# A four-layer graph attention kernel: five small edits in its last layer

## The chip, the cores and the metric

The kernel runs on one core of a Trainium2 chip. The metric is the time of one execution in microseconds of the device. Before the change the median of four runs is 2012.05 us (2011.6 to 2016.34).

A core has engines with a queue of instructions each, worked off in order: PE (matrix products), DVE (VectorE, element-wise), ACT (ScalarE, activations), POOL (GpSimd) and SP (only starts transfers here). They meet through semaphores. A transfer is started by an instruction in the queue of SP, ACT or POOL, and is then carried by 16 DMA engines.

## The reference

x is 4096 nodes by 256 features, adj a 4096 by 4096 matrix of zeros and ones with about 17 ones in a row. Four layers follow each other, each of the form

```python
x = layernorm(x + gat(x, adj, weights))
```

Layers 0 to 2 are graph attention with 4, 4 and 2 heads. Layer 3, the only one that the change touches, is

```python
h = x @ W
e = leaky_relu(h @ a[:256] + (h @ a[256:]).T, 0.2)
attention = softmax(where(adj > 0, e, -1e12))
negative = -softmax(where(adj > 0, -e, -1e12))
new = concatenate([attention @ x, negative @ x], axis=1) @ fc_W
x = layernorm(x + elu(new))
```

## The kernel before

**Two kinds of rows.** The 4096 rows are 32 tiles of 128. A first stage has turned adj into lists of the nodes that a tile's rows are joined to. In layer 3 the tiles 0 to 24 (`self.order`) go by such lists, "listed tiles" here: the values of the listed nodes, 516 numbers a node (two heads of 257, and two more), are gathered from DRAM by GpSimd, one indirect DMA for 128 nodes (`RowTile.load`, L802), and the masked weights are multiplied with them. The tiles 28 to 31 and then 25 to 27 (`WHOLE[3]`) go over all 4096 nodes instead, "all-node rows": `Layer.whole_rows`.

**A listed tile** has two halves. Half 0 takes its own rows (loaded by SP, L797) and 6 gathers, half 1 takes 7. A half is done by `RowTile.half`: ACT makes relu and two exponentials (L879, L880, L882), DVE masks the two weight tiles (L881 for head 1, then L883 for head 0), PE multiplies (L933). Its lists are of two sorts: a list in `FULL` serves all 128 rows of the tile, of the two lists of an entry in `PAIRS` one serves the first 64 rows and the other the last 64, and their matmuls run side by side on the left and the right half of the array. Half 0 has 1 full list and 3 pairs, half 1 has 3 full lists and 2 pairs. Each f32 matmul is two passes in the trace, so a half is 28 passes in both cases. The order of half 0 of layer 3 is: head 1 full, head 1 pairs, head 0 full, head 0 pairs. The buffers for the gathered rows (`g0`, `g1`, four each) hold two tiles in layer 3, so the gathers of half h of tile m wait until half h of tile m-2 has been multiplied. The last tile's half 1 is done list by list in `last_half` (L943 to L950).

**All-node rows** are worked off in units: one unit is one block of 128 nodes and one head for the 4 or 3 tiles of a group; SP loads the block's values (`vw`, L1193), ACT and DVE make the weights (`pw`, L1208 to L1213), PE has 4 or 3 matmuls (L1216). Layer 3 has 128 units, 64 for each group; 10 (`AHEAD`) are done while layer 2 ends, the others are spread by `Layer.whole` over the half steps (`step` counts halves of listed tiles, 50 in all, `count` is 25):

```python
while self.between is None and self.used < self.total \
        and self.used < self.ahead + (self.total - self.ahead) * (step + 1) / (2 * self.count - 6):
    self.unit()
```

After its last unit a group's tiles are finished one by one (`finish`, L1381 to L1389: division, elu, residual), each with its features loaded by `load_x` just then.

**The norm** (`norm`, L1318 to L1349) gathers tiles into a group (`GROUPS`) and takes the inverse root for the whole group: by three Newton steps on DVE (14 small operations), or, if the tile is the last listed one, by one `pow` on GpSimd (L1331). Tiles are normed in the order in which they are finished, listed and all-node ones mixed: a group of 25 and 23 comes, then one of 26, 27 and 24.

**Stores.** `scale` puts finished rows into `self.outs`; `store_rows` (L1094) starts their stores from ACT's queue. `half_with_whole` calls it in each half step after that half's first exponential, if something waits there, and `close` calls it before and after the last tile's `finish`.

**The order of the instructions** on an engine is not that of the Python text: a scheduler in the framework places each instruction by its own estimate, so an edit may move instructions that it does not name. The engines keep that order strictly.

Of the kernel before, what the change touches and what calls it, by code (L numbers as in the profile page):

```python
# [50 lines left out]
P = 128  # L51
N = 4096
F = 256
NT = N // P
# [4 lines left out]
JG = 8  # L59
# [20 lines left out]
FULL = ((0,), tuple(range(NPAIR - FIRST, NPACK - FIRST)))  # L80
PAIRS = (tuple(range(1, 1 + FIRST)), tuple(range(NPAIR - FIRST)))
# [680 lines left out]
class RowTile:  # L762
# [77 lines left out]
    def half(self, half):  # L840
        L, n, nc = self.layer, self.layer.n, self.layer.nc
        prog, sh, S = L.prog, L.shared, self.S
        H, Wd, V, T, A = HEADS[n], WIDTH[n], VALS[n], TERMS[n], LOGS[n]
# [3 lines left out]
        accs, U = self.accs, UNITS[half]  # L847
# [72 lines left out]
            turns = ((3, 0), (1, 2)) if n < 2 else ((0,), (1,))  # L920


        for t, heads in enumerate(turns):
            for us in (FULL[half], PAIRS[half])[::-1 if t == 1 and (half == 1 or n < 3) else 1]:
                for h in heads:
                    for u in us:
                        for rows, g in parts[u]:
                            a = accs[h][rows, :Wd] if n == 3 else accs[0][rows, h * Wd:(h + 1) * Wd]
                            b = g[:, h * Wd:(h + 1) * Wd]
                            if n < 2:  # L930
                                a = accs[0][rows, h * Wd:(H + 1) * Wd].rearrange("p (s c) -> p s c", c=Wd)[:, ::H - h]
                                b = b.rearrange("p (s c) -> p s c", s=1).to_broadcast([P, 2, Wd])
                            nc.tensor.matmul(a, w[h][:, u, rows], b,  # L933
                                             start=half == 0 and u == 0 and (n == 3 or h == turns[0][0]),
                                             stop=half == 1, skip_group_check=True)

    def last_half(self, accs, parts, w, mh):

# [21 lines left out]
class Layer:  # L960
# [39 lines left out]
    def whole(self, step):  # L1000

        while self.between is None and self.used < self.total \
                and self.used < self.ahead + (self.total - self.ahead) * (step + 1) / (2 * self.count - 6):
            self.unit()
        if self.used == self.total:
            next(self.units, None)
# [83 lines left out]
        self.stored = projs  # L1090

    def store_rows(self):
        for y, m in self.outs:
            self.nc.scalar.dma_start(out=self.prog.out[m * P:(m + 1) * P, :], in_=y)  # L1094
        self.outs = []

    def steps(self):
# [13 lines left out]
    def close(self, following):  # L1111

        last = self.count - 1
        self.step += 2
        for proj in self.stored:
            proj.store()
        if self.middle is not None:
            self.middle.values()
            self.middle.edge()
            self.middle.store()  # L1120
        for entry in [e for e in self.ready if e[2] < MIX]:
            self.ready.remove(entry)
            self.set_banks()
            Projection(self.prog, self.n + 1, self.nxt, *entry[1:]).all()
        if following is not None:
            for m in range(4 if following.n == 3 else 2 if WHOLE[self.n] else 1):
                following.load(m, 0)
        if WHOLE[self.n]:
            for _ in self.units:
                pass  # L1130
            if following is None:
                self.store_rows()
                self.tile(last).finish()
                self.store_rows()
                return


            self.closing = True
            following.ahead = AHEAD
            self.project_ready()  # L1140
            for _ in range(3):
                following.unit()
            self.tile(last).finish()
            scaled = self.scaled
            proj = self.project_ready()
            with ExitStack() as order:
                for ins in (scaled, proj.last):
                    order.enter_context(self.prog.tc.issue_after(ins.ins))
                following.tile(0).half(0)
                for _ in range(AHEAD - 3):  # L1150
                    following.unit()
                following.tile(1).half(0)
        else:
            self.set_banks()
            first = Projection(self.prog, self.n + 1, self.nxt, *self.ready.pop(0)[1:])
            first.transpose()
            following.tile(0).half(0)
            first.copy()
            first.multiply()
            first.values()  # L1160
            self.tile(last).finish()
            first.edge()
            first.store()
        self.project_ready()
        if following is not None:
            for m in (1, 2):
                following.load(m, 0)
            if not WHOLE[self.n]:
                following.tile(1).half(0)
            following.load(3, 0)  # L1170


    def whole_rows(self):
        n, nc, prog, sh = self.n, self.nc, self.prog, self.shared
        H, Wd, T = HEADS[n], WIDTH[n], TERMS[n]
        groups = [range(H)] if n < 3 else [(0,), (1,)]
        for tiles in WHOLE[n]:
            g = len(tiles)
            S = prog.bk.tile([P, T, BT, P], F32, name="Sw")
            for it, m in enumerate(tiles):  # L1180
                nc.sync.dma_start(out=S[:, :, it, :], in_=sh["e"][n][m].partition_broadcast(P))
            bits = self.block_bits(tiles)
            zs = [None] * g
            for heads in groups:
                accs = [prog.bank(prog.pfour) for _ in range(g)]
                c0, c1 = heads[0] * Wd, (heads[-1] + 1) * Wd
                vs = {}

                def fetch(j):
                    if j >= NT:  # L1190
                        return
                    vs[j] = prog.vp.tile([P, c1 - c0], F32, name="vw")
                    nc.sync.dma_start(out=vs[j], in_=sh["v"][n][0][j * P:(j + 1) * P, c0:c1])  # L1193

                for j in range(4):
                    fetch(j)
                for j in range(NT):
                    fetch(j + 4)
                    mj = self.bytes(bits, j)
                    v = vs.pop(j)  # L1200
                    for h in heads:
                        p = prog.dp.tile([P, BT, P], F32, name="pw")[:, :g]
                        d = sh["d"][n][:, j, h if n < 3 else 0:h + 1 if n < 3 else 1]
                        if n < 3:
                            nc.scalar.activation(p, S[:, h, :g], AF.Exp, bias=d)  # L1205
                            nc.vector.scalar_tensor_tensor(p, p, LEAST, mj, op0=ALU.max, op1=ALU.mult)  # L1206
                        else:
                            nc.scalar.activation(p, S[:, 0, :g], AF.Relu, bias=d)  # L1208
                            if h == 0:
                                nc.scalar.activation(p, p, AF.Exp, bias=sh["shift2"])  # L1210
                            else:
                                nc.scalar.activation(p, p, AF.Exp, scale=-1.0)  # L1212
                            nc.vector.tensor_tensor(p, p, mj, op=ALU.mult)  # L1213
                        c = h * Wd - c0
                        for it in range(g):
                            nc.tensor.matmul(accs[it][:, c:c + Wd], p[:, it, :], v[:, c:c + Wd],  # L1216
                                             start=(j == 0 and h == heads[0]), stop=(j == NT - 1),
                                             skip_group_check=True)
                    if n == 3 and heads[0] == 0 and j == NT - 1:
                        def between(accs=accs):  # L1220
                            for it in range(g):
                                zs[it], last = self.positive(accs[it], whole=True)
                            return last
                        self.between = between
                    yield
            for it, m in enumerate(tiles):
                self.finish(m, accs[it], self.load_x(m), zs[it])
                if n == 3:
                    yield

# [80 lines left out]
    def norm(self, y, m):  # L1311
# [13 lines left out]

        v = ep.tile([P, BT], F32, name="v")[:, :g]
        nc.vector.tensor_scalar(v, mv[:, :, 1], EPS, None, op0=ALU.add)
        if self.n == 3 and m == self.order[-1]:

            r = ep.tile([P, BT], F32, name="r")[:, :g]  # L1330
            nc.gpsimd.tensor_tensor(r, v, self.shared["mhalf"][:, :g], op=ALU.pow)  # L1331
            self.scale(mv, r)
            return
# [518 lines left out]
```

## Time and profile before

| what | us |
|---|---|
| median of four runs | 2012.05 |
| the profiled execution, its time | 2022.25 |
| the span of its trace (first to last instruction) | 2020.5 |
| first gather of layer 3 in the trace | 1544.72 |
| last gather of layer 3 | 1987.38 |
| last GpSimd operation (the `pow`) | 2007.78 |
| last DVE operation ends | 2009.77 |

Times below are microseconds from the start of the span of the profiled execution, which took 10.2 us more than the median of the runs. In a line of the trace, "L933" is a line of the kernel, PEld is PE's loading of weights, a letter q behind an engine's name (POOLq) means its queue alone was at work, and the brackets at the end give the time that the engine stood idle before and what released it. The view of groups gives busy time, mean nanoseconds of one instruction, and idle time before them. The chain of waits goes back from the last instruction to what released each step.

### The profile page before, as it was taken

Reading aid. Unit: us, or ns where it says so; the run is one execution under the profiler, and the core shown is the slowest. Engines: PE = TensorE matmul, PEld = TensorE weight load, DVE = VectorE, ACT = ScalarE, POOL = GpSimd, SP = SyncE. Lnnn points to the kernel's source line nnn. Section 1 sums busy time; section 2 is a strip of 40 time slices with the busy share of each in tenths; the row PEclk is TensorE's granted clock in tenths of the full one; section 3 lists DMA queues with packets and bytes.
Section 4 is the critical chain, followed back from the end, with each engine's and each line's share of the span. In section 5 each row is a group of like instructions: output and inputs, shape, how many; then the busy total and the mean of one; then the engine's idle time right before and its main releaser. Section 6 shows DMA issues by size and latency. Waiting matters only on the chain. (4 is left out here: it accounts for less than half of the span.)

```text
span 2020.5 us, 46645 instructions
## 1 busy us (share of the span) xinstructions
PE 1776.3 (88%) x15137; PEld 1456.2 (72%) x15137; DVE 1543.9 (76%) x5130; ACT 1494.5 (74%) x4705; POOL 1418.4 (70%) x1413
## 2 busy tenths in 40 slices
PE   5758889988999699999998889798988999999994
PEld 3537677777777589888776688788876777766672
DVE  3458888888888699988887878787866577686765
ACT  4659888899878577876677778777774688777763
POOL 0067777777777777777777777777763777777772
PEclk7759899999999899999999999899998999999997
DMA  8799999999756766666666657667765888898883
GB/s 300 224 337 315 313 288 283 294 296 297 227 170 196 198 175 187 179 185 167 183 171 181 187 160 196 183 188 210 201 184 155 245 274 257 269 294 276 279 264 103
DMA packets 294057, 459.20 MB, mean 227 GB/s; under 512 B 90982, under 2 KB 206795, under 8 KB 293804
## 3 DMA queue, kind: packets, MB, share of 16 engines
q0 software_dynamic: 76544, 233.01, 39.6%
q1 hardware_dynamic: 212642, 218.92, 35.1%
q10 hardware_dynamic: 4618, 4.20, 0.6%
q8 instruction: 122, 2.00, 0.4%
q14 instruction: 131, 1.07, 0.2%
HBM read 407.14 MB, written 48.81 MB: 226 GB/s over the span
## 5 line engine op out<-in xcount | busy, mean ns | idle before, releaser
L802 POOL DMA_INDIRECT G<-vals,idx x1378 | 1413.0, 1025 | 569.8 <-issue 350.7
L933 PE MATMUL bank<-G,w 128*64 128x130 f32 (+5 forms) x9268 | 939.9, 306 | 72.3 <-DVE w L869 66.7
L912 ACT ACTIVATE w<-S,G 128x64 f32<-128x64 f32 (+1 forms) x3108 | 833.9, 351 | 149.5 <-DMA G<-vals,idx 143.2
L933 PEld LDWEIGHTS bank<-G,w 128*64 128x64 f32 (+1 forms) x9268 | 756.1, 157 | 235.1 <-DVE w L869 82.5
L1216 PE MATMUL bank<-vw,pw 128*128 128x129 f32 (+1 forms) x2304 | 375.6, 319 | 19.4 <-ACT zw L1364 4.9
L1216 PEld LDWEIGHTS bank<-vw,pw 128*128 128x128 f32 x2304 | 332.9, 192 | 57.3 <-issue 15.9
L869 DVE SCALAR_TENSOR_TENSOR w<-w,bank 128x1024 f32<-128x1024 f32 (+1 forms) x240 | 322.7, 1345 | 12.9 <-ACT w L912 11.1
L696 PE MATMUL bank<-wext,xT 128*128 128x268 f32 (+3 forms) x640 | 190.3, 433 | 26.7 <-ACT xT L687 25.4
L879 ACT ACTIVATE w<-S,G 128x64 f32<-128x64 f32 (+1 forms) x343 | 108.9, 352 | 77.6 <-DMA G<-vals,idx 59.7
L696 PEld LDWEIGHTS bank<-wext,xT 128*128 128x128 f32 x640 | 125.1, 213 | 53.3 <-ACT xT L687 28.2
L404 ACT ACTIVATE mk<-raw 128x1024 uint8<-128x1024 int32 x128 | 129.6, 1048 | 26.3 <-DMA raw<-in_adjB_dram 25.1
L1206 DVE SCALAR_TENSOR_TENSOR pw<-pw,mw 128x512 f32<-128x512 f32 (+1 forms) x192 | 120.9, 642 | 30.3 <-ACT pw L1205 28.3
L1205 ACT ACTIVATE pw<-Sw,d 128x512 f32<-128x512 f32 (+1 forms) x192 | 126.4, 675 | 15.1 <-PE bank L1216 8.0
L908 DVE TENSOR_TENSOR w<-S,G 128x384 f32<-128x384 f32 x180 | 91.0, 508 | 41.7 <-DMA G<-vals,idx 36.9
L1213 DVE TENSOR_TENSOR pw<-pw,mw 128x512 f32<-128x512 f32 (+1 forms) x128 | 79.1, 621 | 53.4 <-ACT pw L1210 32.1
L1277 PE MATMUL bank<-vw,pw 128*128 128x65 f32 x512 | 89.3, 257 | 15.1 <-DVE pw L1274 15.1
L1279 PE MATMUL bank<-pw,vw 128*65 128x128 f32 x512 | 99.0, 276 | 0.0
L1277 PEld LDWEIGHTS bank<-vw,pw 128*128 128x128 f32 x512 | 78.1, 193 | 23.9 <-issue 21.0
L1208 ACT ACTIVATE pw<-Sw,d 128x512 f32<-128x512 f32 (+1 forms) x128 | 82.9, 655 | 14.9 <-DVE y L1349 6.4
L1274 DVE SCALAR_TENSOR_TENSOR pw<-Sw,cw,mw 128x512 f32<-128x512 f32 x128 | 92.8, 740 | 0.0
L687 ACT COPY xT<-bank 128x256 f32<-128x256 f32 x128 | 45.6, 358 | 57.2 <-PE bank L682 37.5
L914 DVE SCALAR_TENSOR_TENSOR w<-w,mk 128x512 f32<-128x512 f32 (+1 forms) x84 | 62.7, 751 | 23.6 <-ACT w L912 23.5
(197 smaller groups left out, 1912.0 us busy)
## 6 DMA issues: line engine op xcount, KB each, us to landing
raw<-in_adjB_dram SPq DMA_DIRECT2D x128, 512.0 KB
G<-vals,idx POOLq DMA_INDIRECT x1378
vw<-vals SPq DMA_DIRECT2D x128, 128.5 KB
S<-edge SPq DMA_DIRECT2D x60, 256.0 KB
vw<-vals SPq DMA_DIRECT2D x96, 129.0 KB
xp<-y SPq DMA_DIRECT2D x96, 128.0 KB
y<-xp SPq DMA_DIRECT2D x96, 128.0 KB
vals<-row SPq DMA_DIRECT2D x64, 152.0 KB
```

The lines of the kernel that those rows point to most:

```text
L404: nc.scalar.activation(self.mk[:, 2 * q:2 * q + 2], src, AF.Copy)
L696: nc.tensor.matmul(pp[:, :c1 - c0], self.xT[:, k, :], wext[:, k, c0:c1], start=(k == 0), stop=(k == KT - 1 and brow is None))
L802: nc.gpsimd.indirect_dma_start(out=self.row(half, k), out_offset=None, in_=self.values[:N + 1 if half else MIX * P, :].rearrange("r (k c) ...
L869: return nc.vector.scalar_tensor_tensor(pair, pair, LEAST, mh2, op0=ALU.max, op1=ALU.mult)
L879: nc.scalar.activation(w[0][:, u, rows], S[:, 0, rows], AF.Relu, bias=d(g, 0))
L912: nc.scalar.activation(w[h][:, u, rows], S[:, h, rows], AF.Exp, bias=d(g, h))
L933: nc.tensor.matmul(a, w[h][:, u, rows], b, start=half == 0 and u == 0 and (n == 3 or h == turns[0][0]), stop=half == 1, skip_group_check=True)
L1205: nc.scalar.activation(p, S[:, h, :g], AF.Exp, bias=d)
L1206: nc.vector.scalar_tensor_tensor(p, p, LEAST, mj, op0=ALU.max, op1=ALU.mult)
L1216: nc.tensor.matmul(accs[it][:, c:c + Wd], p[:, it, :], v[:, c:c + Wd], start=(j == 0 and h == heads[0]), stop=(j == NT - 1), skip_group_ch ...
L1277: nc.tensor.matmul(bu[:, it * Wd:(it + 1) * Wd], p[up][:, it, :], v[:, up * Wd:(up + 1) * Wd], start=j == 0 and it == 0, **how)
L1279: nc.tensor.matmul(bf[:Wd, it * P:(it + 1) * P], v[:, flat * Wd:(flat + 1) * Wd], p[flat][:, it, :], start=j == 0 and it == 0, **how)
```

## The change

Five things change:

- In `half`, half 0 of layer 3 multiplies head 1 full, head 0 full, head 1 pairs, head 0 pairs. All other halves keep their order.
- In `whole`, the divisor for layer 3 is `2 * count - 8` in place of `2 * count - 6`: its units are used up two half steps sooner.
- In `whole_rows`, the features of a group's tiles are loaded 8 units before the group's end, not at the finish.
- In `norm`, the `pow` on GpSimd is taken for the last two listed tiles, 23 and 24, with what stands in the group with them.
- In `store_rows`, every second store goes by SP's queue when `closing` is set; `close` now sets it for the last layer too.

```diff
-        for t, heads in enumerate(turns):
-            for us in (FULL[half], PAIRS[half])[::-1 if t == 1 and (half == 1 or n < 3) else 1]:
-                for h in heads:
+        runs = [(us, heads) for t, heads in enumerate(turns) for us in (FULL[half], PAIRS[half])[::-1 if t else 1]]
+        if n == 3 and half == 0:
+            runs = [(us, heads) for us in (FULL[0], PAIRS[0]) for heads in turns]
+        for us, heads in runs:
+            for h in heads:
...
-                and self.used < self.ahead + (self.total - self.ahead) * (step + 1) / (2 * self.count - 6):
+                and self.used < self.ahead + (self.total - self.ahead) * (step + 1) / (2 * self.count - (8 if self.n == 3 else 6)):
...
     def store_rows(self):
-        for y, m in self.outs:
-            self.nc.scalar.dma_start(out=self.prog.out[m * P:(m + 1) * P, :], in_=y)
+        for k, (y, m) in enumerate(self.outs):
+            queue = self.nc.sync if self.closing and k % 2 else self.nc.scalar
+            queue.dma_start(out=self.prog.out[m * P:(m + 1) * P, :], in_=y)
...
             for _ in self.units:
                 pass
+            self.closing = True
             if following is None:
                 self.store_rows()
                 self.tile(last).finish()
                 self.store_rows()
                 return
-
-
-            self.closing = True
...
-            zs = [None] * g
+            zs, ys = [None] * g, []
...
+                    if heads == groups[-1] and j == NT - JG:
+                        ys = [self.load_x(m) for m in tiles]
...
-                self.finish(m, accs[it], self.load_x(m), zs[it])
+                self.finish(m, accs[it], ys[it], zs[it])
...
-        if self.n == 3 and m == self.order[-1]:
+        if self.n == 3 and m in self.order[-2:]:
```

More of the change, by code (lines that the diff above doesn't have):

```diff
@@ L920, in half @@
             turns = ((3, 0), (1, 2)) if n < 2 else ((0,), (1,))
-        for t, heads in enumerate(turns):
-            for us in (FULL[half], PAIRS[half])[::-1 if t == 1 and (half == 1 or n < 3) else 1]:
-                for h in heads:
[L926 to L935, printed above, removed]
+        runs = [(us, heads) for t, heads in enumerate(turns) for us in (FULL[half], PAIRS[half])[::-1 if t else 1]]
[3 more added lines that the diff above has]
+            for h in heads:
+                for u in us:
+                    for rows, g in parts[u]:
+                        a = accs[h][rows, :Wd] if n == 3 else accs[0][rows, h * Wd:(h + 1) * Wd]
+                        b = g[:, h * Wd:(h + 1) * Wd]
+                        if n < 2:
+                            a = accs[0][rows, h * Wd:(H + 1) * Wd].rearrange("p (s c) -> p s c", c=Wd)[:, ::H - h]
+                            b = b.rearrange("p (s c) -> p s c", s=1).to_broadcast([P, 2, Wd])
+                        nc.tensor.matmul(a, w[h][:, u, rows], b,
+                                         start=half == 0 and u == 0 and (n == 3 or h == turns[0][0]),
+                                         stop=half == 1, skip_group_check=True)
     def last_half(self, accs, parts, w, mh):
```

## The prediction

> **What bounds the kernel now.** Only layer 3 is in question: up to it the compiled order of both programs is the same on every engine. I read first the busy time by stages. Columns: us, then busy (x instructions) of PE, PEld, DVE, ACT, POOL, PE's clock, DMA share, GB/s.
>
> ```profile
> 1720.00:1760.00 40.00, 40.00 (x217) 30.35 (x216) 26.93 (x92) 27.54 (x64) 29.01 (x30) 1.00 0.87 267
> 1800.00:1840.00 40.00, 39.88 (x222) 29.04 (x220) 28.19 (x111) 30.64 (x73) 30.59 (x31) 1.00 0.89 283
> 1990.00:2010.50 20.50, 4.31 (x17) 1.78 (x12) 16.01 (x73) 4.91 (x14) 0.89 (x1) 0.74 0.10 33
> ```
>
> PE looks like the bound until 1960, and after 1990 DVE works almost alone for 20 us. But POOL's groups, asked for before and after 1770, tell more:
>
> ```profile
> L802 POOL DMA_INDIRECT G<-vals,idx x123 | 127.3, 1035 | 43.7 <-issue 28.6 <-PE bank L933 4.9 <-ACT w L879 3.8
> L802 POOL DMA_INDIRECT G<-vals,idx x166 | 168.8, 1017 | 50.6 <-issue 38.7 <-DMA G<-vals,idx 4.0 <-PE bank L933 3.4
> ```
>
> Idle time for each gather is 43.7/123 = 0.36 us and 50.6/166 = 0.30. The timeline shows 0.30 between any two gathers, so before 1770 POOL really waited for 43.7 - 123 x 0.30 = 6.8 us, and after 1770 for nothing: it goes from gather to gather at (168.8 + 50.6)/166 = 1.32 us. The last real waits are these:
>
> ```profile
> 1747.78 0.94 POOL L802 DMA_INDIRECT G<-vals,idx  x1 [1.97 <-ACT e L1387]
> 1765.29 0.94 POOL L802 DMA_INDIRECT G<-vals,idx  x1 [0.70 <-ACT z L1364]
> ```
>
> 1747.78 is the first gather of tile 11. It needs the buffers of tile 9, whose half 0 PE ends at 1747.48 (chain: 1743.51 + 3.97), 0.3 us earlier; the releaser named is only what came last. So until tile 12 POOL is let go by PE, then it runs free, and the last gathers close the chain of waits. There (start, us, what):
>
> ```profile
> 1987.38 4.02 DMA G<-vals,idx
> 1991.42 0.40 ACT w L943
> ...
> 2003.21 0.73 DVE y L1349 x2
> ...
> 2007.74 0.49 POOLq L167
> 2008.23 0.45 POOL r L1331
> ```
>
> From the last gather to the last root are 2007.78 - 1987.38 = 20.4 us. The landing takes 4; the rest is DVE, which finishes rows 25 to 27 and tile 23 before it comes to tile 24. And what ends the span is not the stores: by the view of line 1848 POOL drains after its last operation,
>
> ```profile
> L1848 POOLq DRAIN  x3: 44/107/8730, 2011.0 to 2020.3; - x3
> ```
>
> 8.73 us from 2011.0, while the other engines' first drains stand at 2013.8 at the latest. The time is POOL's last root plus 2020.5 - 2007.78 = 12.7 us.
>
> **The change part by part.**
>
> *Order of half 0.* Passes of full lists and of all-node units take 0.217 us each (18 in 3.90), a pair's two passes together the same. Four full passes and 12 x 0.217 for the pairs make 3.47. The chain shows 3.97 for half 0 and then 4.10 for the next 18 passes instead of 3.90. So there are 0.50 + 0.20 us in two changes from full to pairs and two back. The new order has one of each: -0.35 us for each of 25 halves. Head 0's full list now stands ahead of all pairs, so all wait for DVE's second mask product (L883). Its cover was head 1's 12 pair passes, some 1.5 us; now it is 0.43 us. It hides as long as weights lie ready: L883 for a half 0 starts at 1640.36, PE takes one at 1652.3; the next are 1665.38 and 1669.8. I take no cost.
>
> *Units two steps sooner.* 118 units over 42 half steps in place of 44: 2.81 for 2.68. In the compiled order, PE has 256 all-node matmuls ahead of tile 9's half 1, before it had 244. 12 x 0.433 = +5.2 us, less 8 halves (tiles 2 to 9; the first two fall into stalls) x 0.35 = 2.8: PE frees that buffer 2.4 us later. The gather that needs it (tile 11, half 1) started at 1755.37, 0.45 ahead of that half's end at 1755.82; others (1611.05 and 1612.24) start 1.2 ahead of it, since the first of its two buffers is free by then. So 0.7 us were in hand: +1.7. Tile 12's first gather waited 0.4, so it moves by +1.3, and as POOL runs free from there, so does the last gather: **+1.3 us**. This edit alone makes the gathers later. Ends: -2.8 (only the switches count), +5.2 (only the units).
>
> *What it gives is behind the last gather.* By the compiled order, rows 25 to 27 are now divided and finished around the halves of tiles 23 and 24, between their mask products. Norm groups become 25 with 22, 26 and 27 with 23, and 24 alone. I set the rows' durations into the new order, the landings unchanged. ACT's last exponential ends at 1992.75 as before. DVE reaches L883 of tile 24's half 0 at 1986.7 instead of 1984.88 (other rows' steps stand ahead of it), then waits until 1989.4 for an exponential that ACT has placed behind a landing, and ends its last mask product at 1993.5. PE ends at about 1995.2, not late. Then:
>
> - tile 23: z 0.48, two L1349 0.73, minimum 0.29; its exponential stands behind two stores on ACT (0.34 + 0.39) and ends at 1995.6; then 0.43 + 0.46 + 0.20 + 0.20 and its root at 1997.1;
> - root 0.89 and three L1349 1.06: DVE is free for tile 24 at 1999.0;
> - tile 24: from L1381 to the root 2007.78 - 2003.86 = 3.92: its root at 2002.95.
>
> That is 4.85 us sooner: **-4.85**. The 14 Newton steps for tile 23 (1999.99 to 2003.18, 3.2 us) are within it: they are gone from this place, and those of 25 and 22 run in gaps of tile 24's products. If DVE meets no wait at the landing, it is 1.5 more; if it falls one more exponential behind, 1.5 less. GpSimd's added root (0.89 us, nearest row L1331) starts after the last gather: nobody queues behind it but the last root.
>
> *Features sooner.* Seven loads of 128 KB. The scheduler had hoisted them already: in the compiled order of SP the run of five loads of y moves by a few places only, and no finish at 1990 to 1998 waits for a transfer. Nothing; were one late, some 4 us (a gather's landing) would hit rows 25 to 27, whose finish is not last any more.
>
> *Two queues.* No store stands in SP's compiled order: when the last `store_rows` runs, tile 24 alone is left, and number 0 goes by ACT. Even before, the three last issues (0.34 to 0.41 us each) lay beside POOL's drain. Nothing, either way.
>
> A rule against the change: the Trainium skill, "SBUF — State Buffer", section "SBUF: two separate sides", says that a DVE operation in a two-port mode locks GpSimd out while it writes descriptors. The trace has gathers of 0.942 to 1.554 us, so something does stretch them; 10 us of DVE work moves from after the gathers to beside them. By the page each of some 15 wide operations could hold one gather for its 0.4 us, an estimate of 6 us at most, and the sum would be 2.5 us slower.
>
> By rows: from 1920 to 1990 POOL spent 52.5 us on 53 gathers, 2.4 over 53 x 0.945, beside 43.4 us of DVE; 10 more make +0.55. I leave it in the range.
>
> **Sum.** -4.85 + 1.3 = -3.55 us. The span falls from 2020.5 to 2016.95; the profiled time of 2022.25 stands 10.2 above the median, and the difference in us is carried over: 2012.05 - 3.55 = 2008.5.
>
> **Rivals.**
>
> 1. *Gathers not later.* PE's savings pay in full, or POOL meets fewer stretched gathers: 0 to -2.8. For it: PE has 100% in the stage where POOL waits for it. Against: 12 more matmuls. 2012.05 - 4.85 - 0 to 2.8 = 2004.4 to 2007.2.
> 2. *The units eat the gain.* The switches save little or DVE stretches gathers: +3 to +5.2 gives 2010.2 to 2012.4.
> 3. *Slower.* Half 0's pairs wait for L883. From L881 to L883 are 0.68 to 1.4 us from start to start, 0.43 are covered: 0.3 to 1.0 us lost where PE takes weights as they come, and 1.8 where DVE has other rows between (2.2 from start to start at 1774.52). It decides once L883 ends later than PE's arrival + 0.43 on tiles 2 to 10, where POOL is let go by PE: 9 x 1 to 9 x 2 us on top of 2008.5, 2017 to 2026. Against: leads of 4 to 11 us above. And after 1770, where leads are small, POOL hides it.
> 4. *It does not do what it says.* DVE's row of small steps swallows the tail's gain: tile 24's root is still behind tile 23's, and if DVE's last mask product came at 1996 instead of 1993.5, with gathers +1.3: 2011.
>
> **How the numbers follow.** A measurement tells about 0.2%, 4.0 us: faster is under 2008.0. Forecast 2008.5 with 0.50 (its own range 2006.5 to 2010.5; half of it below 2008.0); rival 1 0.23; rival 2 0.12; rival 3 0.09; rival 4 0.06. Faster: 0.25 + 0.23 = 0.48. Same: 0.25 + 0.12 + 0.06 = 0.43. Slower: 0.09. The range goes from rival 1's end, 2004.4, to rival 2's 2012.4 and 0.6 for stretched gathers: 2004.4 to 2013.0.
>
> **What would show it.** Half 0 in the chain: 3.97 becomes 3.6 or so. POOL's real waits before 1770 grow from 6.8 to 8 us, and its last gather starts at about 1988.7. Two roots on GpSimd at the end, some 6 us apart, the last at 2004.2; the drain again 8.7. All 32 stores on ACTq. If the last gather starts sooner than 1987.4, the step on the units is wrong; if the distance from last gather to last root is not 15 to 16 us, that on the tail; if PE idles within half 0 for DVE's L883, rival 3 has come.

## The result, and the profile after

The changed kernel took 2017.08 us (median of 44 runs), the kernel before 2013.81 (median of 69): the ratio is 1.0017, 95% interval 1.0009 to 1.0024. That is slower by about 3.4 us, where 3.55 us less was forecast, and outside the range. (The 2012.05 of the forecast was the median of four runs of the kernel before.) Each ratio here and below is to runs of the kernel before on the same chip in the same round: its median was 2012.9, 2014.7 and 2019.0 us in three rounds, so ratios can be compared between rounds and microseconds can't.

The two profiled executions say the opposite: spans of 2016.3 us after and 2020.5 before. They can't be compared as wholes: single executions of the kernel before differ by up to 16 us (2006.5 to 2022.7). The first gather of layer 3 stands at 1532.44 after and 1544.72 before, 12.3 us apart, while the instructions and their order are the same on every engine up to there; PE's first differ some 20 us later. Over the 14 profiles of this study that point lies between 1531.4 and 1544.8. (The two of the kernel before are the latest; but if 12 us were the change's own, the changed kernel would be faster, and the timed runs say slower.) So I count from the first gather of layer 3:

| from the first gather of layer 3, us | before, two profiles | changed, three profiles |
|---|---|---|
| to tile 12's first gather | 220.6, 219.6 | 226.3, 224.3, 221.2 |
| from there to tile 12's first gather of half 1 | 7.8, 7.6 | 13.6, 13.0, 13.4 |
| from there to the last gather | 214.2, 216.9 | 214.8, 215.2, 214.5 |
| from the last gather to the end of the span | 33.1, 32.8 | 29.1, 28.4, 29.1 |
| sum | 475.8, 477.0 | 483.9, 480.9, 478.2 |

(The third changed profile is that of a kernel with the same order of instructions, `late_loads` below.) By the means of the rows, +3.8 up to tile 12, +5.6 in one step, -0.7 behind it, -4.1 in the tail: +4.6 us, of the size of the measured +3.4. The tail's gain came; the gathers lost twice as much.

GpSimd's groups, before and after 1773.5, answer to those of the forecast before and after 1770 (line, engine, operation, count, busy us, mean ns, idle before and its releasers):

```profile
L802 POOL DMA_INDIRECT G<-vals,idx x118 | 122.8, 1041 | 52.8 <-issue 28.6 <-PE bank L935 17.8 <-ACT w L879 3.0
L802 POOL DMA_INDIRECT G<-vals,idx x162 | 165.3, 1020 | 49.5 <-issue 36.3 <-DMA G<-vals,idx 4.0 <-PE bank L935 3.7
```

Behind 1773.5 it is as before: 49.5 - 162 x 0.30 = 0.9 us beyond the usual distance. Ahead of it 52.8 - 118 x 0.30 = 17.4 us of real waits, where before had 6.8. One of them is large. GpSimd's timeline there (start, us, line, operation, count, idle before and releaser):

```profile
1749.20 1.32 POOL L802 DMA_INDIRECT G<-vals,idx  x1 [2.50 <-PE bank L935]
...
1765.18 0.95 POOL L802 DMA_INDIRECT G<-vals,idx  x1 [0.30 <-issue]
1772.40 0.98 POOL L802 DMA_INDIRECT G<-vals,idx  x1 [6.27 <-PE bank L935]
```

1772.40 is the first gather of tile 12's half 1. It needs a buffer of tile 10's half 1, which PE is only then multiplying. PE's timeline at the same place:

```profile
1751.67 2.34 PE L935 MATMUL bank<-G,w 128*64 128x257 f32 x20
1761.19 1.20 PE L1217 MATMUL bank<-vw,pw 128*128 128x257 f32 x2 [7.18 <-issue]
1763.27 1.20 PE L1217 MATMUL bank<-vw,pw 128*128 128x257 f32 x2 [0.88 <-DVE zw L1386]
1765.66 1.20 PE L1217 MATMUL bank<-vw,pw 128*128 128x257 f32 x2 [1.19 <-DVE zw L1386]
1766.65 6.94 PE L935 MATMUL bank<-G,w 128*128 128x257 f32 x28
```

PE ends tile 10's half 0 at 1754.01 and then idles 7.18 + 0.88 + 1.19 = 9.25 us. What it waits for is the first unit of the **second all-node group**: three matmuls (two records each), one for each of rows 25 to 27, into banks that still hold the sums of the first group. DVE must divide these sums out (L1386) first. (A "bank" is a buffer in which PE adds up its products.) Behind the three stands tile 10's half 1, the last line, ready or not. The releaser of the 7.18 is only given as "issue"; DVE's timeline names the operation:

```profile
1759.66 0.56 DVE L1214 TENSOR_TENSOR pw<-pw,mw 128x384 f32<-128x384 f32 x1 [3.16 <-ACT pw L1211]
...
1760.61 0.48 DVE L1386 SCALAR_TENSOR_TENSOR zw<-bank,rec,zw 128x256 f32<-128x256 f32 x1
...
1762.65 0.47 DVE L1386 SCALAR_TENSOR_TENSOR zw<-bank,rec,zw 128x256 f32<-128x256 f32 x1
...
1765.04 0.47 DVE L1386 SCALAR_TENSOR_TENSOR zw<-bank,rec,zw 128x256 f32<-128x256 f32 x1
```

The divisions end at 1761.09, 1763.12 and 1765.51, and PE's three steps start 0.10 to 0.15 us after each. DVE came to the first so late because a weight product (L1214) stands ahead of it in the queue, which waited 3.16 us for ACT. And ACT's row says what held ACT:

```profile
1758.48 0.64 ACT L879 ACTIVATE w<-S,G 128x128 f32<-128x128 f32 x2 [2.83 <-DMA G<-vals]
1759.03 0.60 ACT L1211 ACTIVATE pw<-pw,shift 128x384 f32<-128x384 f32 x1
```

It is the landing of tile 11's own rows, with nothing of the first group in it. Four engines' queues in a row hand the delay on.

In the kernel before, the same switch stands one half later, behind tile 10's half 1:

```profile
1764.91 4.95 PE L933 MATMUL bank<-G,w 128*128 128x257 f32 x28
1769.70 1.10 PE L1216 MATMUL bank<-vw,pw 128*128 128x257 f32 x4
1773.29 0.67 PE L1216 MATMUL bank<-vw,pw 128*128 128x257 f32 x2 [2.49 <-DVE rec L1381]
1773.80 5.72 PE L933 MATMUL bank<-G,w 128*128 128x257 f32 x28
```

There PE had two halves to multiply in the meantime and lost 2.49 us; and the half behind the wait is tile 11's half 0, which ended at 1779.52, while GpSimd wanted its buffers only at 1783.07 (tile 13's first gather).

In the tail, that is from the last gather to the end of the span, the forecast's rows came nearly as worked out (GpSimd's two roots, then its drain):

```profile
1996.63 0.90 POOL L1334 TENSOR_TENSOR r<-v,mhalf 128x3 f32<-128x3 f32 x1 [8.45 <-DVE v L1330]
2003.34 0.56 POOL L1334 TENSOR_TENSOR r<-v,mhalf 128x1 f32<-128x1 f32 x1 [5.81 <-DVE v L1330]
```

```profile
L1851 POOLq DRAIN  x3: 44/107/8730, 2006.8 to 2016.1; - x3
```

From the last gather (1987.23) the last root is 16.1 us away (forecast 15 to 16, before 20.4), and the end 29.1 us.

### The profile page after: what moved, and what is told of

The parts are those of the page before. It is cut to its first block, busy times and chain, and to the rows that moved or that the text cites. A ratio compares the mean times of both kernels' runs of the same rounds, so it can differ in the third digit from the quotient of the medians.

```text
span 2016.3 us, 46629 instructions
## 1 busy us (share of the span) xinstructions
PE 1768.9 (88%) x15137; PEld 1460.1 (72%) x15137; DVE 1538.2 (76%) x5116; ACT 1493.7 (74%) x4705; POOL 1412.1 (70%) x1414
## 5 line engine op out<-in xcount | busy, mean ns | idle before, releaser
L912 ACT ACTIVATE w<-S,G 128x64 f32<-128x64 f32 (+1 forms) x3108 | 833.5, 351 | 143.6 <-DMA G<-vals,idx 135.1
L1217 PE MATMUL bank<-vw,pw 128*128 128x129 f32 (+1 forms) x2304 | 381.3, 322 | 23.7 <-issue 9.2
L1217 PEld LDWEIGHTS bank<-vw,pw 128*128 128x128 f32 x2304 | 337.5, 195 | 63.2 <-issue 24.6
L1214 DVE TENSOR_TENSOR pw<-pw,mw 128x512 f32<-128x512 f32 (+1 forms) x128 | 79.2, 621 | 54.3 <-ACT pw L1211 32.0
L1280 PEld LDWEIGHTS bank<-vw,pw 128*128 128x128 f32 x512 | 78.1, 193 | 23.9 <-issue 21.8
```

Of the source, the lines that this page charges most:

```text
L912: nc.scalar.activation(w[h][:, u, rows], S[:, h, rows], AF.Exp, bias=d(g, h))
L1280: nc.tensor.matmul(bu[:, it * Wd:(it + 1) * Wd], p[up][:, it, :], v[:, up * Wd:(up + 1) * Wd], start=j == 0 and it == 0, **how)
```

## The experiments

**Theory A**: the switch of the all-node groups now stands ahead of tile 10's half 1, and GpSimd, let go by that half, waits with it. **Theory B**: there is no such place; 12 more matmuls ahead of tile 9's half 1, and what goes with them, delay the gathers little by little. **Theory C**: the stretch varies from run to run, and one profile shows nothing. **Theory D** is on the end: GpSimd's drain, not the stores, is what comes last. The edits are against the changed kernel unless it is said otherwise. All stretches in one table, one profile each (us; "step" is from tile 12's first gather to its half 1; the ratios of the runs below are from 12 executions each, six for ramp68_newton):

| kernel | to tile 12 | step | first to last gather | last gather to end | ratio to before (95%) |
|---|---|---|---|---|---|
| before | 220.6 | 7.8 | 442.7 | 33.1 | |
| before_again | 219.6 | 7.6 | 444.1 | 32.8 | 0.9993 (0.9978 to 1.0008) |
| changed | 226.3 | 13.6 | 454.8 | 29.1 | 1.0017 (1.0009 to 1.0024) |
| after_again | 224.3 | 13.0 | 452.5 | 28.4 | 1.0026 (1.0009 to 1.0043) |
| late_loads | 221.2 | 13.4 | 449.0 | 29.1 | 1.0010 (0.9993 to 1.0026) |
| units_6 | 216.9 | 7.9 | 440.8 | 31.7 | 0.9991 (0.9975 to 1.0008) |
| units_7 | 221.2 | 7.7 | 446.6 | 30.6 | 1.0009 (0.9991 to 1.0027) |
| hold | 222.3 | 7.9 | 444.1 | 28.4 | 0.9994 (0.9977 to 1.0011) |
| units_only | 225.8 | 14.3 | 453.4 | 30.8 | 1.0023 (1.0002 to 1.0045) |
| one_root | 224.8 | 12.9 | 454.3 | 30.9 | 1.0025 (1.0009 to 1.0041) |
| old_order | 226.6 | 12.2 | 454.7 | 29.3 | 1.0021 (1.0003 to 1.0038) |
| hold_newton | 225.1 | 7.9 | 446.2 | 25.2 | 0.9982 (0.9963 to 1.0002) |
| ramp68_newton | 218.0 | 7.9 | 440.9 | 25.9 | 0.9941 (0.9920 to 0.9962) |
| ramp48_newton | 217.8 | 8.1 | 443.1 | 29.6 | 0.9962 (0.9947 to 0.9977) |

**What one profile is worth.** Both kernels unchanged, once more.

> The changed kernel once more, for what differs from run to run. Measured between the first and the last gather of layer 3: 442.7 us in the profile of before, 454.8 in that of the changed kernel; from the last gather to the end of the span: 33.1 and 29.1. Theory A (a wait of TensorE at the switch of the all-node groups now stands ahead of tile 10's half 1, and GpSimd's gathers of tile 12 wait for that half): again 452 to 457, with a gap of 5 us or more on GpSimd ahead of tile 12's half 1. Theory C (that stretch differs by some us from run to run, and one profile of each says little): not within 2 us of 454.8, and the gap is not there. Time 1.001 to 1.0025 of before by both.

> The kernel before once more, as a second profile of it. Measured in its first profile: 442.7 us from the first to the last gather of layer 3, 228.4 to the first gather of tile 12's half 1, no gap of over 2 us ahead of that, and 33.1 from the last gather to the end. If single profiles can be compared in these stretches: 441 to 445, 226 to 231 and 32.5 to 34. If not: off by 5 us or more. Time 0.999 to 1.001.

The stretch to tile 12 moves by up to 5 us between profiles of one order of instructions, the step by 0.6, the tail by 0.7. So C falls for the step and the tail, and holds in part for the slow loss ahead of tile 12, if it is counted from the first gather.

There is a later event to count from: PE's start on tile 1's half 1. Ahead of it PE has the same halves and units in both programs; only the passes within half 0 of tiles 0 and 1 stand in the new order. Of the 5.1 us between the two outermost profiles of the changed order, 3.3 have come up by then. So here is the slow loss counted from that event. Before, then changed:

```profile
1607.39 4.85 PE L933 MATMUL bank<-G,w 128*128 128x257 f32 x28
1750.97 4.84 PE L933 MATMUL bank<-G,w 128*128 128x257 f32 x28
```

```profile
1597.03 4.84 PE L935 MATMUL bank<-G,w 128*128 128x257 f32 x28
1742.00 3.71 PE L1217 MATMUL bank<-vw,pw 128*128 128x257 f32 x16 [1.23 <-DMA vw<-vals]
1745.55 8.46 PE L935 MATMUL bank<-G,w 128*128 128x257 f32 x56
```

The last line of each is where PE starts tile 9's half 1, which frees the buffer for tile 11's half 1.

| from PE's start of tile 1's half 1, us | to PE's tile 9, half 1 | to tile 12's first gather |
|---|---|---|
| before, before_again | 143.6, 143.6 | 157.9, 157.9 |
| new order of half 0 alone (units_6, ramp68_newton) | 140.8, 140.8 | 154.7, 154.8 |
| units sooner alone (old_order, units_only) | 148.8, 149.9 | 161.6, 162.8 |
| both (changed, after_again, late_loads) | 148.5, 148.6, 147.0 | 161.7, 161.8, 159.9 |

Alone, the new order takes 2.8 us off and the units put 5.2 (old_order) or 6.3 on. Together they put 3.4 to 5.0 on where the forecast had 2.4, so a good part of what the order saves is lost again. It goes in waits of PE ahead of all-node matmuls. The largest are for a block's values (`DMA vw<-vals`): 1.23 us in the line above, 2.2 in two waits in after_again, none in late_loads, which has the least loss.

**Where the switch stands.** Two divisors:

```diff
-  / (2 * self.count - (8 if self.n == 3 else 6)):
+  / (2 * self.count - 6):                            # units_6
+  / (2 * self.count - (7 if self.n == 3 else 6)):    # units_7
```

> The changed kernel with the old divisor (2 * count - 6): the switch of the groups is behind tile 10's half 1 again, and 244 all-node matmuls stand ahead of tile 9's half 1, not 256; the new order of half 0, two roots on GpSimd, sooner loads and two queues stay. Theory A: first to last gather 439 to 443 us, no gap of over 2 us ahead of tile 12's half 1. Theory B (the 12 more matmuls make the gathers later, little by little): 446 to 450, since the switches saved stay. The distance from last gather to end grows, as rows 25 to 27 come later again: 30 to 34 us. Time 0.997 to 1.000 by A, 1.000 to 1.002 by B.

> Divisor 2 * count - 7: as many all-node matmuls (256) ahead of tile 9's half 1 as in the changed kernel, or nearly, but the switch of the groups falls behind tile 10's half 1 as before the change. Theory A: first to last gather 443 to 448 us, and no gap of over 2 us ahead of tile 12's half 1. Theory B: as the changed kernel, 452 to 456. Last gather to end 29 to 32. Time 0.998 to 1.000 by A, 1.001 to 1.002 by B.

With 6 the step is 7.9 and the stretch 440.8; with 7, which has 252 matmuls ahead of tile 9's half 1 (one unit fewer than the changed kernel's 256) and the switch behind tile 10's half 1, the step is 7.7 and the stretch 446.6. Both lie in A's bounds, and units_7 speaks against B. Its time is no clear gain (1.0009, where A gave 0.998 to 1.000): GpSimd there waits 3.61 us one half further on, ahead of tile 13.

**The wait alone.** The first unit of the second group is held until tile 10's half 1 is issued, and the order of the compute instructions changes only around tiles 10 and 11: the first four units of that group (12 matmuls) then stand together ahead of tile 11's half 0.

```diff
-        while self.between is None and self.used < self.total \
+        while self.between is None and self.used < self.total and not (self.n == 3 and self.used == 68 and step < 21) \
```

> The changed kernel, with the first units of the second all-node group held until tile 10's half 1 has been issued; every unit ahead of it and all that follows tile 11 are in the places of the changed kernel. Theory A: the gap ahead of tile 12's half 1 goes, first to last gather 447 to 450 us (some 6 less than the changed kernel, the 3.6 lost up to tile 11 stay); last gather to end 29 as there; time 6 us below the changed kernel, 0.998 to 0.9995 of before. Theory B: 453 to 456, and time as the changed kernel, 1.001 to 1.0025.

The step falls from 13.0 and 13.6 to 7.9; the tail stays. The stretch is 8.4 to 10.7 us shorter than in the changed kernel's first two profiles, of which 5.1 to 5.7 are the step; at 444.1 it is below the 447 to 450 that A gave. Its median time is 5.4 us below that of after_again in the same round (2012.98 and 2018.42; 95% interval of the difference some 1 to 12 us). PE still waits at the switch:

```profile
1759.29 0.67 PE L1217 MATMUL bank<-vw,pw 128*128 128x257 f32 x2 [0.42 <-PE bank L935]
1761.32 0.67 PE L1217 MATMUL bank<-vw,pw 128*128 128x257 f32 x2 [1.36 <-DVE zw L1386]
1763.70 7.38 PE L1217 MATMUL bank<-vw,pw 128*128 128x257 f32 x20 [1.71 <-DVE zw L1386]
```

but 3.5 us and not 9.25, with tile 10's half 1 already behind it, and GpSimd goes on without a gap:

```profile
1764.29 1.02 POOL L802 DMA_INDIRECT G<-vals,idx  x1 [0.30 <-issue]
```

Theory A is shown for the step. The loss ahead of tile 12, which is of B's kind and the smaller one, is not touched by this edit.

**The parts one by one.** The units alone in the kernel before; the changed kernel with one root on GpSimd; the changed kernel with the old order of half 0.

```diff
+  / (2 * self.count - (8 if self.n == 3 else 6)):    # units_only: in the kernel before
-        if self.n == 3 and m in self.order[-2:]:
+        if self.n == 3 and m == self.order[-1]:       # one_root
-        if n == 3 and half == 0:                      # old_order
-            runs = [(us, heads) for us in (FULL[0], PAIRS[0]) for heads in turns]
```

> Before with the divisor alone changed (8 for layer 3): the units two steps sooner, the old order of half 0, one root on GpSimd. Measured so far from the first to the last gather of layer 3: before 442.7 us, changed kernel 454.8 and 452.5, with the old divisor 440.8. Theory A (the switch of the groups stands ahead of tile 10's half 1): 455 to 459, with a gap of 4 us or more ahead of tile 12's half 1; time 1.002 to 1.005 of before. Theory B (a gradual loss from 12 more matmuls, no gap): 446 to 450. The last gather to the end by the forecast's step on the tail, which gives the whole gain to rows 25 to 27 coming sooner: 29 to 30 us where two roots are not needed for it, 31 to 33 where they are.

> The changed kernel with GpSimd's root for the last tile alone; tile 23 with 26 and 27 goes back to Newton's steps on VectorE. First to last gather as the changed kernel, 452 to 455. Last gather to end: if the second root carries the tail's gain, 31.5 to 33 (the 3.2 us of 14 steps return); if the rows that come sooner carry it, 28.5 to 30.5. Time 1.001 to 1.004 of before.

> The changed kernel with half 0's old order of passes (four changes of tile shape, not two). By the forecast, 0.35 us in each half 0 ahead of tile 10 return: from the first gather to that of tile 11's half 0, 2.5 to 3.5 us more than the 205.3 and 206.7 of the changed kernel; first to last gather 455 to 458. If the order's saving is eaten by waits for weights (the third rival), no more, 452 to 455. Time 1.002 to 1.004 or 1.001 to 1.0025.

The divisor alone makes the step of 14.3 us; the stretch is 453.4, a little under A's 455. For the tail, the truth lies between the two readings: rows 25 to 27 coming sooner give 33.0 - 30.8 = 2.2 us, the second root about 2 more (one_root's 30.9 against the 29.1 and 28.4 of the changed kernel). The old order of half 0 has tile 11's first gather at 208.9 us, the changed kernel at 206.7, 205.3 and (late_loads) 203.2: 2 to 6 us, but with a spread of up to 5 between profiles of one order. Counted from PE's tile 1, tile 12's first gather shows 0 to 3 us of it (161.6 and 162.8 against 159.9 to 161.8), and at the last gather nothing is left (454.7 against 454.8; 455 to 458 was expected). The reason is not the one that the expectation names, weights that come late: from the start of its first pass to the end of its last, half 0 takes at most 4.13 us in old_order and 3.78 in the changed kernel for tiles 2 to 10, so the saving is made in every half, and lost in the waits for all-node blocks above.

**Loads and stores.** The features are loaded at the finish again, and all stores go by ACT.

```diff
-                    if heads == groups[-1] and j == NT - JG:
-                        ys = [self.load_x(m) for m in tiles]
...
-                self.finish(m, accs[it], ys[it], zs[it])
+                self.finish(m, accs[it], self.load_x(m), zs[it])
...
-            queue = self.nc.sync if self.closing and k % 2 else self.nc.scalar
-            queue.dma_start(out=self.prog.out[m * P:(m + 1) * P, :], in_=y)
+            self.nc.scalar.dma_start(out=self.prog.out[m * P:(m + 1) * P, :], in_=y)
```

> The changed kernel with the features loaded at the finish again, and all stores from ScalarE's queue. By the forecast both edits are worth nothing: 452 to 455 us from first to last gather, 28 to 30 from there to the end, time 1.001 to 1.003 of before. If the sooner loads carry part of the tail's gain, it is 30 to 33; if they crowd the queue of the all-node rows, first to last gather is 2 us or more shorter.

Compiled, this kernel has the same instructions in the same order as the changed one on all five engines; only some of DVE's waits are named otherwise. Its shorter stretch (449.0, where 452 to 455 was expected) is therefore no evidence that the sooner loads crowd a queue; it is one more sample of what differs from run to run. Beside the other three edits, these two change nothing that is executed.

**The end, and a better version.** No root of layer 3 on GpSimd, once in `hold` and twice with another spread of the units.

```diff
-        if self.n == 3 and m in self.order[-2:]:
+        if False:
```

```diff
-  (8 if self.n == 3 else 6)
+  ((min(8, max(6, 6 + (step - 21) / 8))) if self.n == 3 else 6)    # ramp68; ramp48 has 4 for 6
```

> The kernel with the second group held, and no root of layer 3 on GpSimd: all are Newton's steps on VectorE, so that GpSimd has nothing to do behind the last gathers. First to last gather as with the group held, 443 to 448. Theory D (GpSimd's drain of 8.73 us, which begins only behind its last root, sets the end): the drain lies beside the tail, and the end comes with the last store, 22 to 26 us from the last gather, not 28.4; time 0.996 to 0.998 of before. Its rival (the drain, or what follows, waits for the other engines and comes last wherever the root is): 28 to 31 us, and 0.999 to 1.001.

> The changed kernel with the old divisor until tile 10 is through, then a ramp from 6 to 8 over 16 half steps, and no root of layer 3 on GpSimd: the units stand as before the change up to tile 12, the switch is behind tile 10's half 1, and the last units come two steps sooner. Theory A and D together: 440 to 443 us from first to last gather as with the old divisor, 25 to 26 from there to the end as with Newton's steps, some 466 in all against 475.8 in before's profile; time 0.995 to 0.997. If units that come faster behind tile 12 hold GpSimd there, 444 to 448, and 0.997 to 0.999.

> As the kernel with the ramp from 6 to 8, but with divisor 4 until tile 10 is through: 8 fewer all-node matmuls ahead of tile 9's half 1, and the switch one half later, behind tile 11's half 0. If the number of units ahead is what holds GpSimd until tile 11 (0.43 us each), 196 to 198 us from the first gather to that of tile 11's half 0, against 199.8 with divisor 6, and first to last 438 to 441; if the switch at tile 11 then holds it, 441 to 446. Last gather to end 25 to 28, time 0.9945 to 0.998.

In `hold_newton` GpSimd's drain starts at 1982.7 by the view of its line, beside the tail, and with 11.3 us is over at 1994.1, long before the last row is ready (2004 us), though Newton's 14 steps for tile 24 take 2.7 us and the root took 0.56:

```profile
L1851 POOLq DRAIN  x3: 44/113/11335, 1982.7 to 2009.2; - x3
```

The end comes 25.2 us behind the last gather and not 28.4: theory D holds, by profiles: the ratio of 0.9982 is not clear of 1. `ramp68_newton` is: old places up to tile 12, the switch behind tile 10's half 1, the last units two steps sooner, no root on GpSimd. 440.9 + 25.9 = 466.9 us from the first gather, against 475.8 and 477.0 before, and 0.9941 (six executions): it beats both kernels, the changed one through `late_loads`, which has the same order and 12.6 us more in the same round (2019.78 and 2007.14). Fewer units ahead (`ramp48_newton`) bring no sooner gathers at tile 11 (200.4 us, 200.8 with 6; 196 to 198 was expected); PE waits 1.42 us for ACT (L1367) ahead of a run of all-node matmuls on the way there, and single profiles don't tell how much more is chance. They give back 3.7 us in the tail (29.6; 25 to 28 was expected): the last all-node matmul stands 14 us ahead of the last gather and not 25.

## Why the prediction was wrong

- **What bounds the kernel**: right. The end is the last gather plus a tail that ends with GpSimd's drain, and the last gather hangs on PE up to tile 12.
- **Order of half 0**: right. Half 0 is 3.62 us in the chain, not 3.97. units_6, which has it without the sooner units, has PE at tile 9's half 1 2.8 us sooner, counted from tile 1's half 1, and 2.8 was the forecast. The third rival did not come: no wait of PE for L883 is listed between 1600 and 1800 in the changed kernel. That its 2017 is close to the measured 2017.08 is luck.
- **Units two steps sooner: the step that failed.** It put "+1.3" on tile 12's first gather and went on "as POOL runs free from there, so does the last gather". The count was sized well: units_only is 5.2 to 6.2 us later than before at tile 12's first gather, forecast 5.2. Two things were not. First, PE came to tile 9's half 1 not 2.4 us later but 3.4 to 5.0, since it now waits ahead of all-node matmuls, and the sum has no such wait: what one edit saves and the other costs can't be added as if PE were always busy. (The 1.1 us thought to be in hand behind it are there: tile 12's first gather is 2.0 to 3.9 us later, counted the same way, where 1.3 was forecast; from layer 3's first gather it is 3.8 by the means.) Second, and larger, "free from there" is false by one half: GpSimd still needs PE for tile 12's half 1, and the switch of the groups had moved ahead of the half of tile 10 that frees it. That term, +5.6 us, is missing from the sum. The compiled order of PE had it in plain sight, as did the 2.49 us that PE lost at the switch before. I counted the matmuls ahead of one half, and did not ask what stands directly ahead of each half that GpSimd waits for. With +3.8 in place of the forecast's +1.3, and the term that is missing, the sum is -4.85 + 3.8 + 5.6 = +4.55, the other sign.
- **The tail**: right in sum, -4.1 by the means and -4.85 forecast. I left open how much of it belongs to the second root: about 2 us.
- **Features sooner, two queues**: right, nothing, and shown by the compiled order and not only by the time.
- **Stretched gathers**: from tile 12's half 1 to the last gather it takes 214.5 to 215.2 us, before 214.2 and 216.9. The +0.55 worked out from rows can't be told from nothing. Of the estimate of up to 6 us from the Trainium skill's "SBUF — State Buffer", section "SBUF: two separate sides", nothing is seen; the measurement decides.
- **The second rival** named the right side of the sum ("the units eat the gain"), by a weaker mechanism and with bounds up to 2012.4. No rival had a wait that moves.

**What stays open**: why the block's values land too late for PE ahead of tile 9's half 1 in some executions and not in others; and why the part ahead of layer 3 differs by 13 us from profile to profile.

## What to carry to other kernels

When work is moved ahead on an in-order engine, don't sum its length alone: list the waits that travel with it, and look what each now stands in front of. A wait that is covered by two halves of other work in one place costs 2.5 us, and one half sooner 9.25, and the part that counts is what the bound engine is waiting for behind it. Where runs differ by several us ahead of the changed part, count from the last event that stands behind the same work in both programs: PE's start on tile 1's half 1 separated here what layer 3's first gather left in the noise.

## What the hardware showed unexpectedly

GpSimd's drain at the end takes 8.73 us in all 11 profiles in which it starts behind the last root, and 11.3 us (hold_newton), 12.9 us (ramp68_newton) and 13.2 us (ramp48_newton) where it starts beside the last gathers; the other engines' drains take 7 to 123 ns. So with the two roots on that engine, of which the last takes 0.56 us, the end comes 3.2 us later behind the last gather than with Newton's steps on DVE, which take 2.7 us for tile 24 (hold and hold_newton, one profile each; the tails of one order differ by 0.7). The Trainium skill, "VectorE: DVE Perf Modes", section "The DRAIN you can't avoid", has the drains at a program's end at about 12 ns on all engines; the rows are near that for four of the engines (7 to 17 ns in 10 of the 14 profiles, single ones of 110 to 123 ns in the others) and far from it for GpSimd.
